# Reading a batch's edge scores out of an interleaved tile: a four-layer graph network on one Trainium2 core

## The chip, the cores and the metric

The kernel runs on one core of one Trainium2 chip (trn2). The metric is device microseconds of one execution, the median of three. The program is one launch; its input is in DRAM and so is its output.

## The reference, cut to what matters

Four graph layers run one after the other on `x`, which is 16 batches of 1024 nodes with 256 features, float32. All four use one 1024 by 1024 matrix `adj` that is mostly zeros (a random pattern, made symmetric, with the diagonal).

```
# layer 0
pre_u = h @ W1[:d];  pre_v = h @ W1[d:]
hidden = relu(pre_u[:, :, None, :] + pre_v[:, None, :, :] + b1)
S   = sigmoid(hidden @ W2 + b2)                      # (16, 1024, 1024): one score per batch and edge
a_t = einsum('buv,bud->bvd', S * A_a, h)             # the scored sums
m_t = einsum('uv,bud->bvd', A_m, h) * h
z   = beta1*h + beta2*(a_t @ Wa + ba) + beta3*(m_t @ Wm + bm)
# layer 1
z   = z + relu((A @ z) @ W.T + b)
# layers 2 and 3
feats = z @ W1.T;  f1 = feats @ W2 + b2
coefs = softmax(leaky_relu(f1[:, :, None] + f1[:, None, :]) + adj)
z   = coefs @ feats + bias2 + z
```

The change is in the line of `a_t`, the scored sums. `S * A_a` is zero where `adj` is zero, so the kernel works the scores out for the edges alone.

## The kernel before, in words

The 16 batches are worked in four groups of `GB` = 4. All matrices are cut into tiles of `P` = 128 nodes, so there are `NT` = 8 tiles of nodes.

A first stage finds for every node u the places and weights of its edges (up to 32) and makes, for the four batches of a group side by side, the two halves of the hidden layer, `u_d` and `v_d`, and `hw_d`, which is `h @ Wa`. If every node has few enough edges, the arm that starts at line 688 runs; the other arm (`arm.Else`) is a fallback that works on all pairs and isn't taken here.

The order of the work in that arm is written out by hand. Two streams are issued together by Python generators:

- The **side stream** (`score_steps`) makes the scores. One step gathers, for 128 nodes and one edge slot, the row of `v_d` of the neighbour (POOL, line 708), adds the row of u and multiplies (DVE, lines 825 and 827), sums over the features by four ACT activations (line 831), and at the end of a tile takes the sigmoid and multiplies by the edge's weight. Then the scores are scattered (POOL, line 713) into `dense`, a DRAM array of one row for each pair (u, v). **A row holds the four scores of the group's four batches, next to each other: 4 floats, 16 bytes.** There are two such arrays, for alternate groups.
- The **main stream** is the rest. For each group it is `with_edges` (the scored sums, and the only user of `dense`), and then `group_layers` (layers 1 to 3 of that group). `group_layers` of one group runs while the scores of the next one are made. Before the first group, the main stream does what needs no scores (`score_free`). After the last group's `with_edges` come `far_ahead` and `pair_layers`.

How far the side stream goes for each microsecond of the main stream is a constant of the place (`PACE`). `paced(ins, back)` makes an instruction wait for the matmul that was issued `back` products ago, so that no engine runs ahead of the plan. `product` is the helper through which nearly all matmuls go, at line 131, so that they all have this line in the profile.

**The scored sums, `with_edges`.** The output has the features on the partitions: for each batch i and half eh of the features, `acc[i][eh]` is a PSUM bank with 256 columns (`QN`), one for each node v of a block. There are four blocks of columns for each group, and for each block eight tiles `ut` of source nodes. One round of the inner loop takes one tile:

1. `load_gd` (line 907, issued by SP) brings the scores of 128 nodes u and 256 nodes v from `dense` into `gd`, a tile of 128 x 256 x 4 floats, in which the four batches are interleaved as in DRAM. The load is paced 24 products back, three rounds, and waits for the scatters of its group. The pool `gd` has four buffers.
2. ACT copies `gd` into `gc`, 128 x 4 x 256, in which each batch's 256 scores lie next to each other (line 1129). It reads every fourth float. It is paced 16 products back, two rounds. The pool `gc` has two buffers.
3. Eight products follow: for each of four batches and two halves, the stationary operand is a 128 x 128 piece of `hw[i]` and the moving operand is the 256 columns `gc[:, i, :]`. The profile shows two MATMUL and two LDWEIGHTS instructions for each product.

After eight rounds DVE adds the eight banks onto `z` (line 1152). Also issued in these rounds: loads of `z` and, in the first group, loads of the transposed `adj` and its exponential on ACT (line 1118). The first four `gd` tiles of a group are loaded ahead, while the layers of the group before it still run (`soon`).

In all there are 4 groups x 4 blocks x 8 tiles = 128 rounds, so 128 copies and 1024 products.

After the last `with_edges`, `by_lists` takes four tiles of the pool `gd` for another use (`msg`).

Of the kernel before, what the change touches and what calls it, by code (L numbers as in the profile page):

```python
# [11 lines left out]
F32 = mybir.dt.float32  # L12
I32 = mybir.dt.int32
U32 = mybir.dt.uint32
AF = mybir.ActivationFunctionType
ALU = mybir.AluOpType
AX = mybir.AxisListType
P = 128

GB = 4  # L20
# [23 lines left out]
def after(tc, ins, others, kind, why):  # L44
    dep = mybir.DependencyInfo(kind, mybir.DependencyReason.DATA)
    for o in others:
        tc.add_manual_dep(ins.ins, o.ins.name, dep, reason=why)
# [23 lines left out]
def gnn_stack_kernel(  # L71
# [27 lines left out]
    nc = tc.nc  # L99
# [6 lines left out]
    QN = HN // 2  # L106
# [6 lines left out]
    def bank():  # L113
        return psum[-1].tile([P, HN], F32, tag="bank", name="bank")

    def psum_pool(stack, name, bufs):
        psum.append(stack.enter_context(tc.tile_pool(name=name, bufs=bufs, space=bass.MemoryType.PSUM)))
        return psum[-1]
# [4 lines left out]
    def paced(ins, back=6):  # L123


        if recent:
            after(tc, ins, [recent[max(0, len(recent) - back)]], mybir.DependencyClass.Sync, "keeps pace")
        return ins

    def product(*args, **kw):  # L130
        recent.append(nc.tensor.matmul(*args, **kw))  # L131
        del recent[:-BACK]
        return recent[-1]
# [554 lines left out]
    with tc.If(listed > 0) as arm:  # L688
        with ExitStack() as stack:
# [8 lines left out]
            wide_z = stack.enter_context(tc.tile_pool(name="wide_z", bufs=4, reuse_waits="tile"))  # L698
            wide_t = stack.enter_context(tc.tile_pool(name="wide_t", bufs=5, reuse_waits="tile"))
            psum_pool(stack, "banks", 8)  # L700
            gd_pool = stack.enter_context(tc.tile_pool(name="gd", bufs=4, reuse_waits="tile"))
            gc_pool = stack.enter_context(tc.tile_pool(name="gc", bufs=2, reuse_waits="tile"))
            put = [Scatters(tc, f"scores {g}") for g in range(NGR)]
            finished = []
            TW = NT * (D + 1)
# [198 lines left out]
            def load_gd(g, v, ut, **pace):  # L904
                view = dense[g % BUFS][:DUMP].rearrange("(t p v) b -> t p v b", p=P, v=N)
                gd = gd_pool.tile([P, QN, GB], F32, tag="gd", name="gd")
                ins = nc.sync.dma_start(gd, view[ut][:, v * QN : (v + 1) * QN, :])
                put[g].before(paced(ins, **pace))
                return gd
# [207 lines left out]
            def exponential(jt):  # L1117
                paced(nc.scalar.activation(ea[:, jt, :], ea[:, jt, :], AF.Exp), 16)

            def with_edges(g, hw, z):  # L1120

                doing[0] = "edges"
                for v in range(N // QN):
                    cols = slice(v * QN, (v + 1) * QN)
                    acc = [[bank() for _ in range(DH)] for _ in range(GB)]
                    for ut in range(NT):
                        gd = first_gd.pop(0) if first_gd else load_gd(g, v, ut, back=BACK)
                        gc = gc_pool.tile([P, GB, QN], F32, tag="gc", name="gc")
                        paced(nc.scalar.activation(gc, gd.rearrange("p n i -> p i n"), AF.Copy), 16)  # L1129
                        for i in range(GB):  # L1130
                            for eh in range(DH):
                                product(
                                    acc[i][eh][:, :QN], hw[i][:, ut, eh * P : (eh + 1) * P], gc[:, i, :],
                                    start=ut == 0, stop=ut == NT - 1,
                                )
                        if z_loads and ut % 2 == 0:
                            load, i = z_loads.pop(0)
                            paced(load(i), 12)
                        if (to_load or to_exp) and ut % 2 and v:
                            if v > 1 and to_exp:  # L1140
                                exponential(to_exp.pop(0))
                            if to_load:
                                jt = to_load.pop(0)
                                paced(nc.sync.dma_start(ea[:, jt, :], adjT_d[jt]), 16)
                                to_exp.append(jt)
                        yield 3.4 if g or v else 1
                    if v == N // QN - 1:
                        while to_exp:
                            exponential(to_exp.pop(0))
                    for i in range(GB):  # L1150
                        for eh in range(DH):
                            nc.vector.scalar_tensor_tensor(
                                z[i][:, eh, cols], acc[i][eh][:, :QN], zbias[:, eh : eh + 1], z[i][:, eh, cols],
                                ALU.add, ALU.add,
                            )
# [264 lines left out]
            for g in range(NGR):  # L1420
                hw, z = loaded.pop(0)
                while g not in finished:
                    next(side.steps)
                side.along(with_edges(g, hw, z))
                if g < NGR - 1:
                    side.along(group_layers(g, z))
                else:
                    for _ in far_ahead(z[2:], pair_layers(g * GB, z[:2], layer_one(z[:2]))):
                        pass
                    for _ in pair_layers(g * GB + 2, z[2:], from_lists(z[2:], msg)):  # L1430
                        pass
# [131 lines left out]
```

## Time and profile before

| | |
|---|---|
| median of three runs | 3129.5 us (3126.07 to 3133.56) |
| the profiled execution, its own time | 3142.89 us |
| its span, first to last instruction | 3141.2 us |
| mean granted TensorE clock over the span | 0.995 |
| DVE busy | 2356.0 us, 75% |
| ACT busy | 1943.6 us, 62% |
| POOL busy | 1875.3 us, 60% |
| moved by DMA | 699.96 MB, 223 GB/s in the mean |

PE is TensorE's matmul, PEld its weight load, which overlaps it, and DVE, ACT, POOL and SP are the vector, scalar, GpSimd and sync engines. A row of the profile names the line, the engine, the operation, the tile written and the tiles read, the shapes, the number of instructions, then the busy time in us, the mean ns of one, the idle time of its engine just before them, and what ended that idle time. A busy share is an average over stages with different limits, so a change in one stage is read from that stage's own stretch of time.

The main stream passes through these stretches in the profiled execution: the first stage and `score_free` until 948 us; the scored sums of the four groups at 948.0 to 1069.1, 1501.7 to 1623.0, 2057.0 to 2182.8 and 2615.7 to 2726.2 us; `group_layers` in the three gaps between them, 432.6, 434.0 and 432.9 us long; and the end from 2726.2 to 3141.2 us.

### The profile page before, as it was taken

How to read it: one execution, taken by the hardware profiler on the slowest of the kernel's cores; microseconds unless marked ns; L12 is line 12 of the kernel's file. 1: busy time of each engine (PE TensorE's matmuls, PEld its weight loads, DVE VectorE, ACT ScalarE, POOL GpSimd, SP SyncE). 2: the span in 40 equal slices, each digit the busy share in tenths (PEclk: the TensorE clock that was granted, in tenths of full speed). 3: DMA queues.
4: the chain of work that ended last, by engine and by line, in shares of the span. 5: the costliest groups of instructions: out<-in, count | busy, mean ns of one | idle time of the engine just before them, and what ended most of it. 6: DMA issues, size and time to landing. Idle time of an engine off the chain costs nothing. (4 is left out here: it accounts for less than half of the span.)

```text
span 3141.2 us, 39031 instructions
## 1 busy us (share of the span) xinstructions
PE 3082.3 (98%) x11954; PEld 2182.9 (69%) x11954; DVE 2356.0 (75%) x3191; ACT 1943.6 (62%) x6512; POOL 1875.3 (60%) x1483
## 2 busy tenths in 40 slices
PE   9999999999999999999999999999999999999999
PEld 5444545545547756888775688878558888858888
DVE  7887778678774678999677899967789982157844
ACT  3245555566667876777887677778667764414242
POOL 1156778677674577777566776756777770076600
PEclk9999999999999999999999999999999999999999
DMA  9988898888889776568877765887775565485500
GB/s 322 332 321 311 271 293 270 264 253 243 260 288 332 228 215 203 155 187 291 266 228 203 215 164 165 271 266 235 217 212 167 157 200 168 133 256 159 161 4 28
DMA packets 288420, 699.96 MB, mean 223 GB/s; under 512 B 46141, under 2 KB 141178, under 8 KB 281034
## 3 DMA queue, kind: packets, MB, share of 16 engines
q0 software_dynamic: 128224, 387.80, 42.2%
q1 hardware_dynamic: 132538, 258.46, 24.0%
q10 hardware_dynamic: 27440, 51.13, 4.3%
q8 instruction: 96, 1.57, 0.2%
q14 instruction: 122, 1.00, 0.1%
HBM read 565.83 MB, written 131.41 MB: 222 GB/s over the span
## 5 line engine op out<-in xcount | busy, mean ns | idle before, releaser
L831 ACT ACTIVATE z<-z 128x256 f32<-128x256 f32 x2432 | 979.1, 406 | 543.3 <-DVE z L827 453.1
L825 DVE TENSOR_TENSOR z<-z,u 128x1024 f32<-128x1024 f32 x608 | 738.8, 1220 | 384.3 <-PE bank L131 267.6
L131 PE MATMUL bank<-feats,m 128*128 128x257 f32 x4096 | 909.1, 380 | 1.7 <-ACT feats L1016 1.1
L708 POOL DMA_INDIRECT z<-v_d,slot_v x512 | 663.1, 1295 | 404.6 <-ACT z L831 225.7
L131 PEld LDWEIGHTS bank<-feats,m 128*128 128x128 f32 x4096 | 769.3, 190 | 112.4 <-ACT feats L1016 1.9
L713 POOL DMA_INDIRECT dense_d<-gt,slot_at x512 | 665.3, 1299 | 184.6 <-issue 137.4
L827 DVE SCALAR_TENSOR_TENSOR z<-z,w2r 128x1024 f32<-128x1024 f32 x608 | 737.9, 1220 | 9.0
L131 PE MATMUL bank<-gc,hw 128*128 128x256 f32 x2048 | 456.6, 385 | 22.6 <-ACT gc L1129 13.9
L831 ACT ACTIVATION_READ_ACCUMULATOR z<-z 128x1 f32 x2432 | 461.5, 190 | 0.0
L131 PEld LDWEIGHTS bank<-gc,hw 128*128 128x128 f32 x2048 | 389.9, 192 | 88.8 <-ACT gc L1129 22.4
L131 PE MATMUL bank<-adj_sb,h 128*128 128x512 f32 x1024 | 443.6, 593 | 6.5 <-issue 2.8
L1099 DVE SCALAR_TENSOR_TENSOR m<-rho,tau,adj_sb 128x512 f32<-128x512 f32 x512 | 376.5, 744 | 66.5 <-PE bank L131 62.0
L131 PE MATMUL bank<-adjT_in,y 128*128 128x512 f32 (+1 forms) x960 | 403.7, 581 | 6.2 <-issue 3.8
L131 PEld LDWEIGHTS bank<-adj_sb,h 128*128 128x128 f32 x1024 | 194.6, 190 | 247.5 <-issue 242.0
L131 PEld LDWEIGHTS bank<-adjT_in,y 128*128 128x128 f32 x960 | 182.0, 191 | 221.4 <-issue 207.4
L131 PE MATMUL bank<-w,hT 128*128 128x512 f32 (+1 forms) x1024 | 334.8, 487 | 0.0
L1129 ACT ACTIVATE gc<-gd 128x1024 f32<-128x1024 f32 x128 | 264.9, 2071 | 101.0 <-PE bank L131 68.5
L131 PEld LDWEIGHTS bank<-w,hT 128*128 128x128 f32 x1024 | 194.8, 191 | 141.3 <-issue 122.5
L131 PE MATMUL bank<-g_wT,z 128*128 128x257 f32 x1024 | 231.1, 380 | 1.2 <-ACT st L1325 1.1
L131 PEld LDWEIGHTS bank<-g_wT,z 128*128 128x128 f32 x1024 | 192.0, 190 | 32.5 <-issue 3.3
L708 POOL DMA_INDIRECT z<-v_d,x_node x96 | 122.4, 1275 | 129.5 <-ACT z L831 99.5
L713 POOL DMA_INDIRECT dense_d<-gt,x_at x96 | 125.7, 1309 | 29.3 <-issue 27.4
(169 smaller groups left out, 2319.1 us busy)
## 6 DMA issues: line engine op xcount, KB each, us to landing
gd<-dense_d SPq DMA_DIRECT2D x128, 512.0 KB
dense_d<-zero ACTq DMA_DIRECT2D x64, 512.0 KB
adjT_in<-adjT_d SPq DMA_DIRECT2D x112, 256.0 KB
h<-in_x_dram SPq DMA_DIRECT2D x19, 1024.0 KB
u_d<-st SPq DMA_DIRECT2D x64, 256.0 KB
v_d<-st SPq DMA_DIRECT2D x64, 256.0 KB
hw_d<-st SPq DMA_DIRECT2D x64, 256.0 KB
u<-u_d POOLq DMA_DIRECT2D x32, 512.0 KB
```

Source lines behind the costliest of these rows:

```text
L131: recent.append(nc.tensor.matmul(*args, **kw))
L708: return nc.gpsimd.indirect_dma_start(out=dst, out_offset=None, in_=src[:], in_offset=bass.IndirectOffsetOnAxis(ap=at, axis=0), **how,)
L713: return nc.gpsimd.indirect_dma_start(out=dst[:], out_offset=bass.IndirectOffsetOnAxis(ap=at, axis=0), in_=src, in_offset=None,)
L825: paced(nc.vector.tensor_tensor(z, z, u, ALU.add))
L827: nc.vector.scalar_tensor_tensor(zk, zk, 0.0, w2r[:, None, :].to_broadcast([P, GB, D]), ALU.max, ALU.mult)
L831: nc.scalar.activation(zk[:, c, :], zk[:, c, :], AF.Copy, accum_out=s[:, k, c : c + 1])
L1099: nc.vector.scalar_tensor_tensor(m, r[:, cols], ta[:, kt : kt + 1], ea[:, kt, cols], ALU.max, ALU.mult)
L1129: paced(nc.scalar.activation(gc, gd.rearrange("p n i -> p i n"), AF.Copy), 16)
```

## The change

The copy into `gc` is taken out, with its pool. The products read batch i's scores straight from `gd`: the moving operand is `gd[:, :, i]`, 256 floats of which each lies 16 bytes after the one before it. The pool `gd` gets two more buffers, six in place of four.

```diff
-            gd_pool = stack.enter_context(tc.tile_pool(name="gd", bufs=4, reuse_waits="tile"))
-            gc_pool = stack.enter_context(tc.tile_pool(name="gc", bufs=2, reuse_waits="tile"))
+            gd_pool = stack.enter_context(tc.tile_pool(name="gd", bufs=6, reuse_waits="tile"))
...
                         gd = first_gd.pop(0) if first_gd else load_gd(g, v, ut, back=BACK)
-                        gc = gc_pool.tile([P, GB, QN], F32, tag="gc", name="gc")
-                        paced(nc.scalar.activation(gc, gd.rearrange("p n i -> p i n"), AF.Copy), 16)
                         for i in range(GB):
                             for eh in range(DH):
                                 product(
-                                    acc[i][eh][:, :QN], hw[i][:, ut, eh * P : (eh + 1) * P], gc[:, i, :],
+                                    acc[i][eh][:, :QN], hw[i][:, ut, eh * P : (eh + 1) * P], gd[:, :, i],
                                     start=ut == 0, stop=ut == NT - 1,
                                 )
```

The instructions of PE, DVE, POOL and SP stay the same in number and order. On ACT, the 128 copies are gone and everything else keeps its order. A tile of `gd` and one of `gc` have the same size (4 KB on each partition), so the six buffers take the room of the four and two.

## The prediction

> **What bounds the kernel now.** I read the page's busy times first, then its chain of waits, then the groups of instructions, then the stretches of the scored sums one by one, and last the time line of PE in the one group where nothing else runs.
>
> ```profile
> span 3141.2 us, 39031 instructions
> PE 3082.3 (98%) x11954; PEld 2182.9 (69%) x11954; DVE 2356.0 (75%) x3191; ACT 1943.6 (62%) x6512; POOL 1875.3 (60%) x1483
> ...
> DVE 0%; issue 0%
> ...
> L131 PE MATMUL bank<-gc,hw 128*128 128x256 f32 x2048 | 456.6, 385 | 22.6 <-ACT gc L1129 13.9
> L131 PEld LDWEIGHTS bank<-gc,hw 128*128 128x128 f32 x2048 | 389.9, 192 | 88.8 <-ACT gc L1129 22.4
> ...
> L1129 ACT ACTIVATE gc<-gd 128x1024 f32<-128x1024 f32 x128 | 264.9, 2071 | 101.0 <-PE bank L131 68.5
> ```
>
> PE is busy 98% of the span, so what doesn't shorten or lengthen PE's stream changes little. The chain that ended last holds only the last output piece and says nothing about this stage. The products of the scored sums keep PE busy for 456.6 us; PE is idle 22.6 us ahead of them, 13.9 of it for the copy. The copy costs ACT 264.9 us, but ACT is idle 38% of the span.
>
> ```profile
> 948.00:1069.10 121.10, 113.33 (x513) 96.09 (x512) 63.32 (x78) 103.28 (x208) 50.60 (x44) 1.00 0.89 306
> 1501.70:1623.00 121.30, 114.70 (x515) 97.83 (x514) 75.14 (x95) 105.95 (x246) 66.71 (x58) 0.97 0.81 259
> 2057.00:2182.80 125.80, 117.52 (x514) 99.04 (x513) 77.99 (x92) 104.93 (x243) 75.09 (x62) 0.96 0.81 257
> 2615.70:2726.20 110.50, 110.50 (x515) 97.27 (x514) 14.72 (x36) 62.01 (x31) 0.52 (x1) 1.00 0.48 150
> ```
>
> These are the four stretches (length, busy us of PE, PEld, DVE, ACT, POOL, then granted clock, DMA share, GB/s). Together they last 121.1 + 121.3 + 125.8 + 110.5 = 478.7 us. In the fourth, with no score work beside it, PE never stops:
>
> ```profile
> 2615.68 110.67 PE L131 MATMUL bank<-gc,hw 128*128 128x256 f32 x512
> 2726.19 13.98 PE L131 MATMUL bank<-l1wT,z 128*128 128x256 f32 x64
> ```
>
> The next group of matmuls starts 110.5 us after the first of 512, so one instruction takes 110.5 / 512 = 215.8 ns of PE's stream (the 385 ns of the row are of overlapping instructions), 0.843 ns a column. 2048 of them need 442.0 us without a wait; the stage lasts 478.7, so 36.7 us are waits and a lower clock. That is all that taking out the copy can win. Weight loads of 192 ns fit under 215.8 and are no bound.
>
> **The change part by part.**
>
> *Removed: 128 copies.* ACT loses 128 x 2.071 = 264.9 us that nothing waits for except PE's 13.9 us (and ACT's own successors, the score sums of line 831, which are paced by PE). I credit the 13.9 us and the slower clock and small gaps after such stops, 36.7 - 22.6 = 14.1 us, of which I leave about 3 us to the stops that remain. What remains of the idle time is 22.6 - 13.9 = 8.7 us, put down to issue and DVE: PE's two longest are 5.75 us at 1515.7, where the copy itself waited 4.6 us for a remote event (a score tile that landed late, as I read it), and 2.48 us at 2061.9 for an output piece. So 9 + 3 = 12 us of waits stay, and the gain is 36.7 - 12 = 24.7 us, between 0 and 36.7.
>
> *Added waits.* The products now wait for the load of `gd` where the copy did (17.3 us, 12 times, most of it not passed on to PE). The tile is needed one copy later, about 2.1 us, and the pacing of the load, three rounds or 3 x 16 x 0.2158 = 10.4 us ahead, is unchanged. Behind a PE that waits stand DVE's additions (line 1152) and the paced score work, none of it nearer to the end than PE. On SP the loads of `z`, `adj_sb` and `adjT_in` queue behind `gd`; these loads wait on PE already and keep their order. The buffer of `gd` is now let go by the round's last product, not by the copy; with six buffers that is the round six before, older than the pacing. I cost all this at nothing: the cover is those three rounds. If it went, the price is the landings that ACT saw late, 17.3 + 4.6 = 21.9 us, with 12 us of it already in the sum.
>
> *Changed: where the moving operand lies.* 2048 matmuls read 256 floats that lie 16 bytes apart. No matmul of the trace has such an operand, so the price must be bounded. The nearest row is the copy itself: ACT reading the same tile in the same pattern, against ACT reading 128x1024 floats in a row.
>
> ```profile
> L1129 ACT ACTIVATE gc<-gd 128x1024 f32<-128x1024 f32 x128 | 264.9, 2071 | 101.0 <-PE bank L131 68.5 <-DMA gd<-dense_d 17.3 <-issue 10.2
> L870 ACT ACTIVATE u<-b1r 128x1024 f32<-128x1024 f32 x56 | 58.8, 1050 | 31.5 <-DMA adjT_d<-stage 26.2 <-PE bank L131 4.0 <-DVE z L825 0.8
> L1078 ACT ACTIVATE rho<-rho 128x1024 f32<-128x1024 f32 x32 | 33.4, 1044 | 0.0
> ```
>
> The copy takes 2071 ns, 1.98 times the 1044 of line 1078; line 870 also runs through four rows of 256 and takes 1050, so it isn't the shape. It isn't contention either: in the fourth group, with the other engines nearly silent, the copy's mean is 2063. Between 256 and 1024 packed floats ACT's time grows from 406 to 1044 ns (lines 831 and 1078), 0.831 ns a float: the rate at which PE takes columns, 0.843. ACT wants a float at the same pace as PE and gets it at about half that pace when each is 16 bytes further on. Three values for PE:
> - nothing: 215.8 ns an instruction, 2048 x 0.2158 = 442 us;
> - ACT's ratio: 215.8 x 1.98 = 427.3 ns, 875 us;
> - ACT's extra time per float, (2071 - 1044) / 1024 = 1.003 ns, on 256 columns: 215.8 + 256.8 = 472.6 ns, 968 us.
>
> I take the ratio: the row is the same tile, the same step and the same pace. A price below nothing is excluded, since no other row of 256 columns is faster than this one.
>
> [...]
>
> **The sum.** 875 + 12 = 887 us in place of 478.7: 408 us more. The profiled execution's own 3142.9 us (1.7 more than its span) becomes 3551. The median of the runs stands at 3129.5 / 3142.89 = 0.9957 of it, so 3536 us. With the extra time per float: 968 + 12 - 478.7 = +501, 3644, and 3629 as a median. Outside the stage nothing pays it back: in the three stretches between, PE is busy 431.7 of 432.6, 432.1 of 434.0 and 432.1 of 432.9 us. The score work is issued at fixed places between the matmuls and waits longer with PE, so what is late next is nothing but PE.
>
> **The rivals.**
>
> 1. *PE reads scattered floats at no cost* (faster). [...] Against: ACT, at the same pace, loses half. Time: 442 + 12 - 478.7 = -24.7, that is 3118 and 3105 as a median; with all waits gone -36.7, 3093. It decides as long as an instruction stays below (478.7 - 12) / 2048 = 227.9 ns, 12 ns over today: 5.6% is all that PE's reads may lose.
> 2. *PE loses part*, because fetching the next float overlaps taking the last one better than in ACT. At half of the loss: (215.8 + 427.3) / 2 = 321.5 ns, 658 + 12 - 478.7 = +192, 3335 and 3320 as a median. Nothing in the profile speaks for a certain share; a sixth of the loss, about 252 ns, would give 3180.
> 3. *PE loses more than ACT*, if each of the two MATMUL instructions of a product fetched every float twice: above 3660. The packed row gives no sign of a second fetch.
>
> That the change doesn't do what it says I can exclude: the order of instructions shows ACT without its 128 copies and the same 2048 matmuls on `gd`.
>
> **How the numbers follow.** The forecast has 0.70, rival 1 0.18, rival 2 0.10 and rival 3 0.02. The predicted time is the forecast's 3536. Its own range is 3490 to 3660, from the ratio and the extra time per float, with 15 to 30 us for waits that go or come. The range shown reaches down through rival 2 to 3180 and leaves out rivals 1 and 3, 0.20 together. Measurement can tell 0.2%, 6 us, from no change: of rival 1, 0.17 is faster by more, 0.01 is not; the lowest 0.01 of rival 2 is the same too; the rest, 0.81, is slower.
>
> **What would show it.** The row of 2048 matmuls from `gd`, the four stretches, and above all the fourth group, which has no waits: 512 x 0.4273 = 219 us if the ratio holds, 242 with the extra time per float, 165 for half, 110.5 for nothing. The gaps between the groups should keep 432 to 434 us, ACT's busy time should fall by 265 us, and PE's wait for the copy be gone. A fourth group of 110 us would make the prediction wrong at its main step; gaps that shrink by more than some us would make the step "nothing pays it back" wrong.

## The result, and the profile after

The changed kernel takes 3590.9 us in the median of four runs (3587.9 to 3600.1), against 3127.8 us for the kernel before (four runs, 3124.5 to 3133.6): a ratio of 1.149, 95% interval 1.147 to 1.151. The time forecast was 3536 us. Here and below a ratio is the record's estimate from the single runs and need not equal the quotient of the two medians.

The page of the changed kernel: span, busy times, the chain, and two groups of instructions.

```profile
span 3586.1 us, 38830 instructions
PE 3553.3 (99%) x11954; PEld 2219.4 (62%) x11954; DVE 2364.0 (66%) x3191; ACT 1692.9 (47%) x6384; POOL 1854.9 (52%) x1483
...
DVE 0%; issue 0%
...
L131 PE MATMUL bank<-gd,hw 128*128 128x256 f32 x2048 | 928.5, 632 | 0.0
...
L131 PEld LDWEIGHTS bank<-gd,hw 128*128 128x128 f32 x2048 | 426.7, 209 | 499.4 <-issue 495.9
```

The same 2048 matmuls keep PE busy for 928.5 us in place of 456.6. PE waits for nothing ahead of them any more (0.0 in place of 22.6). ACT has 1692.9 us in place of 1943.6: the copies are gone. That is 250.7 us less, not the 265 that the prediction asks for. The prediction took the copies' own row, 264.9 us; but 13 us of that lies, in the records before, over other ACT instructions, which are still there. It doesn't help, since PE, the engine that bounds the kernel, is busy 99% of a longer span.

The four scored sums of the changed kernel, in the columns of the prediction's second fence (length, busy us of PE, PEld, DVE, ACT, POOL, clock, DMA share, GB/s), with one stretch of `group_layers` between the first two:

```profile
946.30:1178.20 231.90, 231.90 (x514) 106.81 (x513) 65.99 (x79) 46.73 (x180) 49.21 (x49) 1.00 0.51 164
1178.20:1610.80 432.60, 431.64 (x1810) 329.53 (x1809) 396.43 (x540) 312.75 (x1192) 317.75 (x232) 1.00 0.68 207
1610.80:1842.70 231.90, 231.90 (x515) 106.99 (x514) 76.96 (x95) 47.70 (x212) 62.70 (x61) 1.00 0.45 140
...
2275.30:2507.50 232.20, 232.20 (x514) 106.75 (x513) 81.71 (x96) 48.58 (x220) 65.91 (x63) 1.00 0.46 143
...
2940.60:3172.50 231.90, 231.90 (x514) 106.61 (x513) 16.44 (x36) 0.19 (x1) 0.52 (x1) 1.00 0.23 72
```

All four take 232 us, whether score work runs beside them (the first three) or not (the fourth). That alone says that no other engine and no transfer sets the time here. Together they last 927.9 us, 449.2 more than the 478.7 before. The span grew by 444.9, so nothing of it is paid back elsewhere beyond 4.3 us; the stretch between the first two groups is 432.6 us long, as before. One instruction takes 231.87 / 512 = 452.9 ns of PE's stream (first to first of the next group, as the prediction counted), 1.769 ns a column against 0.843.

### The profile page after: what moved, and what is told of

Same layout as the page of the kernel before. It is cut to its first block, busy times and chain, and to the rows that moved or that the text cites. A ratio compares the mean times of both kernels' runs of the same rounds, so it can differ in the third digit from the quotient of the medians.

```text
span 3586.1 us, 38830 instructions
## 1 busy us (share of the span) xinstructions
PE 3553.3 (99%) x11954; PEld 2219.4 (62%) x11954; DVE 2364.0 (66%) x3191; ACT 1692.9 (47%) x6384; POOL 1854.9 (52%) x1483
## 5 line engine op out<-in xcount | busy, mean ns | idle before, releaser
L707 POOL DMA_INDIRECT z<-v_d,slot_v x512 | 654.4, 1278 | 652.4 <-ACT z L830 515.7
L131 PE MATMUL bank<-gd,hw 128*128 128x256 f32 x2048 | 928.5, 632 | 0.0
L131 PEld LDWEIGHTS bank<-gd,hw 128*128 128x128 f32 x2048 | 426.7, 209 | 499.4 <-issue 495.9
L1149 DVE SCALAR_TENSOR_TENSOR z<-bank,zbias,z 128x256 f32<-128x256 f32 x128 | 60.5, 482 | 308.1 <-PE bank L131 307.6
L1167 ACT ACTIVATE y<-bank 128x512 f32<-128x512 f32 x64 | 37.8, 590 | 285.6 <-PE bank L131 285.4
```

Of the source, the lines that this page charges most:

```text
L707: return nc.gpsimd.indirect_dma_start(out=dst, out_offset=None, in_=src[:], in_offset=bass.IndirectOffsetOnAxis(ap=at, axis=0), **how,)
L1149: nc.vector.scalar_tensor_tensor(z[i][:, eh, cols], acc[i][eh][:, :QN], zbias[:, eh : eh + 1], z[i][:, eh, cols], ALU.add, ALU.add,)
L1167: nc.scalar.activation(y[i][:, jt : jt + 2, :], ps.rearrange("p (t d) -> p t d", t=2), AF.Copy)
```

## The experiments

The kernels that differ only in what the matmuls read were run once each, apart from the packed one. For all of them the time per instruction is read from the fourth scored sum, where PE never stops: the time from the first of its 512 matmuls to the first of the next group, over 512. "Beside it" means runs of the kernel before made together with the experiment; their median lies between 3139.5 and 3148.9 us, above the 3127.8 of the result, so an experiment is compared with those.

**Is it the step, or the tile that is read?** ACT still copies, but leaves the batches interleaved, with the buffers of before.

```diff
-                        gc = gc_pool.tile([P, GB, QN], F32, tag="gc", name="gc")
-                        paced(nc.scalar.activation(gc, gd.rearrange("p n i -> p i n"), AF.Copy), 16)
+                        gc = gc_pool.tile([P, QN, GB], F32, tag="gc", name="gc")
+                        paced(nc.scalar.activation(gc, gd, AF.Copy), 16)
...
-                                    acc[i][eh][:, :QN], hw[i][:, ut, eh * P : (eh + 1) * P], gc[:, i, :],
+                                    acc[i][eh][:, :QN], hw[i][:, ut, eh * P : (eh + 1) * P], gc[:, :, i],
```

> ACT still copies each loaded tile into gc, but without turning it, so that the products read every fourth float of a tile that ACT wrote, with the buffers of before. If the price lies in the 16-byte step of the moving operand: 2048 matmuls at about 453 ns, 928 us busy, as in the changed kernel, and 3560 to 3600 us in all; the copy itself falls from 2071 to about 1050 ns. If it lies in reading the tile that the DMA has filled, in the six buffers or in the missing copy: 216 ns an instruction, 442 to 457 us busy, about 3130 us.

Measured: 3593.2 us. Two groups of its profile:

```profile
L131 PE MATMUL bank<-gc,hw 128*128 128x256 f32 x2048 | 928.6, 632 | 0.1
...
L1129 ACT ACTIVATE gc<-gd 128x1024 f32<-128x1024 f32 x128 | 135.3, 1057 | 628.9 <-PE bank L131 397.7 <-issue 231.1
```

With copy and buffers back, the matmuls take the same 928.6 us. Neither the direct read of a loaded tile, nor the six buffers, nor the missing copy has a part in it. And the copy halves, from 2071 to 1057 ns, as soon as it reads in a row: the price has moved from ACT to PE.

**What is taking out the copy worth, without the step?** From the changed kernel, the products read packed floats.

```diff
+                        row = gd.rearrange("p n i -> p (n i)")
...
-                                    acc[i][eh][:, :QN], hw[i][:, ut, eh * P : (eh + 1) * P], gd[:, :, i],
+                                    acc[i][eh][:, :QN], hw[i][:, ut, eh * P : (eh + 1) * P], row[:, i * QN : (i + 1) * QN],
```

> No copy, six buffers as in the changed kernel, but the products read 256 floats in a row of the loaded tile (the scores of the wrong pairs: the values of the scored sums are not the reference's). If the step alone is the price: 216 ns an instruction, 442 us, and what the copy's absence is worth shows by itself: 3093 to 3117 us, forecast 3105. If reading the loaded tile directly is the price: 453 ns and about 3590 us. If the loads become the bound: waits of PE for gd of 15 us or more and 3125 us or above.

Measured: 3119.6 us against 3139.5 for the kernel before beside it, ratio 0.9940 (0.9925 to 0.9954). The row of its matmuls:

```profile
L131 PE MATMUL bank<-gd,hw 128*128 128x256 f32 x2048 | 446.1, 380 | 4.8 <-DVE st L1326 2.4 <-DMA gd<-dense_d 2.0 <-issue 0.2
```

The matmuls are busy 446.1 us, PE is idle 4.8 us ahead of them, 2.0 of that for loads of `gd`. So the gain of removing the copy is real, 14 to 24 us, a little less than the 24.7 us credited; and it is about the most that a way of feeding packed scores can win here, with only 4.8 us of idle time left.

**What does the price go by?** Four kernels change only which 256 floats are read (the values of the scored sums are then not the reference's). What the expectations call a line is 16 bytes on a partition, counted from the start of the tile; the text below calls it a piece. That the price would go by pieces of this size was the author's supposition, which these runs test. The diffs show the new text of the changed places; `...` stands for what is left out. The first two:

```diff
+                        row = gd.rearrange("p n i -> p (n i)")
+                        row = row.rearrange("p (n s) -> p n s", s=2)
...
+                                    ... row[:, i // 2 * QN : (i // 2 + 1) * QN, i % 2],
```

> As the changed kernel, but the products read every second float (8 bytes apart; the scores of the wrong pairs). If what costs is each new 16-byte line, 1.77 ns by the changed kernel, and two floats on a line share it: 0.885 ns a column, about 227 ns an instruction, 464 us, 3125 us in all. If the price grows evenly with the step (0.843 ns at one float, 1.771 at four): 1.152 ns, 295 ns, 604 us, 3265 us. If any step above one float is read at half speed: 453 ns, 928 us, 3590 us.

```diff
+                        row = gd.rearrange("p n i -> p (n i)")
+                        row = row[:, : 3 * QN].rearrange("p (n s) -> p n s", s=3)
...
+                                    ... row[:, :, i % 3],
```

> As the changed kernel, but the products read every third float (12 bytes apart; the scores of the wrong pairs). Four such floats lie on three 16-byte lines. If each new line costs 1.77 ns: 1.33 ns a column, 340 ns an instruction, 696 us, 3355 us in all. If the price grows evenly with the step: 1.46 ns, 374 ns, 766 us, 3425 us. If the step is free below 16 bytes: 216 ns, 442 us, 3105 us.

Then a step of 32 bytes, and pairs of neighbours whose beginnings lie 32 bytes apart:

```diff
+                                    ... hw[i].rearrange("p t d -> p (t d)").rearrange("p (n s) -> p n s", s=8)[:, :, ut],
```

> As the changed kernel, but the moving operand is every eighth float (32 bytes apart) of the tile hw, in place of the scores. If each new 16-byte line costs 1.77 ns and how far the lines lie apart doesn't matter: 453 ns an instruction as at 16 bytes, 928 us, about 3590 us in all. If the price goes on growing with the step: 1.239 ns more than a packed float for four more floats of step, 3.0 ns a column, 770 ns an instruction, some 1577 us, 4230 us. The loads of gd stay, but nothing reads them.

```diff
+                        row = gd.rearrange("p n i -> p (n i)")
+                        row = row.rearrange("p (n s) -> p n s", s=8)
...
+                                    acc[i][eh][:, :QN].rearrange("p (n s) -> p n s", s=2), ... row[:, :, 2 * i : 2 * i + 2],
```

> As the changed kernel, but the products read pairs: two floats in a row, then a gap of six, so that pairs begin 32 bytes apart and each line that is touched is hit twice (the scores of the wrong pairs). If only hits for each line count: 227 ns an instruction, 465 us, 3125 to 3145 us in all, as with every second float. If each jump in the pattern costs what a jump of 16 bytes costs: (0.843 + 1.77) / 2 = 1.31 ns a column, 335 ns, 685 us, 3345 us.

The fourth scored sum on PE's time line (start, length, instructions), of every second float, of every third, of the pairs, and of every eighth:

```profile
2609.66 115.79 PE L131 MATMUL bank<-gd,hw 128*128 128x256 f32 x512
2725.30 13.97 PE L131 MATMUL bank<-l1wT,z 128*128 128x256 f32 x64
```

```profile
2770.01 174.03 PE L131 MATMUL bank<-gd,hw 128*128 128x256 f32 x512
2943.87 13.98 PE L131 MATMUL bank<-l1wT,z 128*128 128x256 f32 x64
```

```profile
2617.66 117.82 PE L131 MATMUL bank<-gd,hw 128*128 128x256 f32 x512
2735.32 9.87 PE L131 MATMUL bank<-l1wT,z 128*128 128x256 f32 x45
```

```profile
2962.53 236.11 PE L131 MATMUL bank<-hw 128*128 128x256 f32 x512
3198.46 11.84 PE L131 MATMUL bank<-l1wT,z 128*128 128x256 f32 x54
```

The difference of the two starts over 512, beside the number of 16-byte pieces that 256 such floats touch:

| moving operand | pieces of 16 bytes | ns an instruction | ns a piece | time, us |
|---|---|---|---|---|
| packed | 64 | 215.8 | (3.37) | 3119.6 |
| every second float | 128 | 225.9 | 1.765 | 3141.3 |
| pairs, 32 bytes apart | 128 | 229.8 | 1.795 | 3151.0 |
| every third float | 192 | 339.6 | 1.769 | 3359.3 |
| every fourth (the change) | 256 | 452.9 | 1.769 | 3590.9 |
| every eighth | 256 | 460.8 | 1.800 | 3616.1 |

The last column compares only roughly: the kernel before took 3139.5 us beside the packed, second and third floats, 3148.9 beside the pairs and the eighth floats, and 3127.8 beside the change. Every second float came 16 us above the total expected and the pairs 6 us above the top of theirs, though their instructions took the 227 ns expected within 3 ns; the totals were reckoned from 3105 us for packed operands, which took 3119.6.

One number describes the table within 2%: an instruction takes 215.8 ns or 1.77 ns for each piece that it touches, whichever is longer. Every third float was the sharpest test, since the three readings were 70 us and more apart: 340 ns was expected by pieces, 374 by an even rise with the step, 216 if only a step of 16 bytes counted; 339.6 came out. Why a piece costs PE this much isn't shown by these runs. What falls: that any step halves the speed (every second float), that the price goes on rising with the step beyond 16 bytes (every eighth), that each jump costs (the pairs). Pieces that begin 32 bytes apart cost 1.7% more than pieces 16 bytes apart (460.8 against 452.9 ns). Every eighth float is also read from another tile, `hw`; but the pairs, read from `gd`, show the same 1.7% over every second float (229.8 against 225.9 ns), which points to the distance and not to the tile.

The size of 16 bytes is borne out too. With pieces of 8 bytes every second float would touch 256 of them, as many as every fourth, but the two took 225.9 and 452.9 ns. With pieces of 32 bytes every fourth would touch 128 and every eighth 256, but they took 452.9 and 460.8 ns.

**Does a weight load pay as well?** The operands are exchanged; the sums come out with nodes on the partitions.

```diff
-                                    acc[i][eh][:, :QN], hw[i][:, ut, eh * P : (eh + 1) * P], gd[:, :, i],
+                                    acc[i][eh][:, :QN], gd[:, eh * P : (eh + 1) * P, i], hw[i][:, ut, :],
```

> As the changed kernel, but with the operands exchanged: the weight load takes 128 of the scores, every fourth float of gd, and the moving operand is 256 packed floats of hw, so that the sums come out with the nodes on the partitions; they are added to z as if they had not been turned, so the values are not the reference's. If a weight load also pays 1.77 ns for each line: 128 x 1.77 = 227 ns in place of 190, hidden or nearly hidden beside 216 ns of matmul, 442 to 480 us, 3105 to 3145 us in all. If a weight load at this step takes twice its time: 380 ns, no longer hidden, 778 us, about 3440 us.

Measured: 3157.0 us, with 3148.9 for the kernel before beside it. Its two groups, and the fourth scored sum on PE's time line:

```profile
L131 PE MATMUL bank<-hw,gd 128*128 128x256 f32 x2048 | 484.4, 399 | 3.7 <-DVE st L1325 1.4 <-DMA gd<-dense_d 1.4 <-DVE z L1149 0.7
L131 PEld LDWEIGHTS bank<-hw,gd 128*128 128x128 f32 x2048 | 481.2, 330 | 6.7 <-DMA gd<-dense_d 2.0 <-issue 1.9 <-DVE z L1149 1.3
```

```profile
2620.91 120.16 PE L131 MATMUL bank<-hw,gd 128*128 128x256 f32 x512
2740.91 13.98 PE L131 MATMUL bank<-l1wT,z 128*128 128x256 f32 x64
```

The weight loads now fill the stage, 481.2 us or 235 ns each, 1.84 ns a float; packed ones took 190. One weight load with its matmul takes 120.0 us / 512 = 234.4 ns in the fourth sum, so the weight load sets the pace in place of the 215.8 ns of the matmul. The total is 12 us above the range of the first reading and the stage 4 us above it; the second reading, 380 ns, is far off. That a weight load pays by the piece, like the moving operand, fits (1.84 against 1.77 ns) but rests on this one step. There are only 128 floats in a load, and 216 ns of matmul hide nearly all of it. Against the 446.1 us of packed operands, the same scores cost 38 us as the stationary operand and 482 (928.5) as the moving one. It is no finished kernel, since the sums would have to be turned back.

**Can the 0.6% be had with packed operands?** Five versions of the kernel before, which all keep a turned copy. First, a third buffer for the copies (the smaller changes that this brings, three tiles loaded ahead and the four tiles of `msg`, are left out of the diff):

```diff
-            gd_pool = stack.enter_context(tc.tile_pool(name="gd", bufs=4, reuse_waits="tile"))
-            gc_pool = stack.enter_context(tc.tile_pool(name="gc", bufs=2, reuse_waits="tile"))
+            gd_pool = stack.enter_context(tc.tile_pool(name="gd", bufs=3, reuse_waits="tile"))
+            gc_pool = stack.enter_context(tc.tile_pool(name="gc", bufs=3, reuse_waits="tile"))
```

> The kernel before with three buffers for the turned copy gc and three for gd (three tiles of a group loaded ahead, not four; the four tiles that are used again at the end come two from each pool). If PE's waits for the copy come from its having only two buffers, so that a copy can't start before the products of two rounds ago are done: PE's 13.9 us of waits for the copy fall under 4 us and the time by 8 to 18 us, to 3112 to 3122 us against 3130. If they come from ACT's other work ahead of the copy, or if the lost fourth load hurts: 3125 us or above, with waits for loads of gd in their place.

Measured: 3141.7 against 3148.9 us, ratio 0.9987 (0.9970 to 1.0003).

```profile
L131 PE MATMUL bank<-gc,hw 128*128 128x256 f32 x2048 | 452.3, 382 | 22.6 <-ACT gc L1129 15.6 <-DVE st L1331 4.2 <-issue 2.3
L1129 ACT ACTIVATE gc<-gd 128x1024 f32<-128x1024 f32 x128 | 263.3, 2068 | 87.6 <-PE bank L131 52.8 <-DMA gd<-dense_d 34.7
```

PE waits 15.6 us for copies, not under 4, so a third buffer alone doesn't help. This doesn't yet clear the two buffers: the copies now wait 34.7 us for loads of `gd`, 17.3 before, since a buffer was taken from there, and the pace still holds each copy back until a product of two rounds ago. The last two versions below keep two buffers and lose most of the waits, which does clear them. Next, every second copy on DVE:

```diff
-                        paced(nc.scalar.activation(gc, gd.rearrange("p n i -> p i n"), AF.Copy), 16)
+                        turning = gd.rearrange("p n i -> p i n")
+                        if ut % 2:
+                            paced(nc.vector.tensor_copy(gc, turning), 16)
+                        else:
+                            paced(nc.scalar.activation(gc, turning, AF.Copy), 16)
```

> The kernel before with every second copy made by DVE in place of ACT (64 copies each). If PE's waits for the copy come from how much ACT has to do in the scored sums (it is busy without a gap at 1040 to 1060 us of the kernel before): these waits fall from 13.9 to under 6 us and the time by 6 to 15 us, 0.2 to 0.5%. If they come from where the copy stands in the queue, behind score work that waits itself: DVE's queue has the same waits, PE waits as long as before, and the time stays within 5 us. DVE's own copy at this step has no row yet: 1.77 ns a float would make it 1.8 to 2.0 us.

Measured: 3136.3 against 3141.8 us, ratio 0.9970 (0.9950 to 0.9989). The matmuls, and the two engines' copies of such tiles, in one profile:

```profile
L131 PE MATMUL bank<-gc,hw 128*128 128x256 f32 x2048 | 452.4, 383 | 22.9 <-ACT gc L1133 9.3 <-DVE gc L1131 5.0 <-issue 4.7
L1133 ACT ACTIVATE gc<-gd 128x1024 f32<-128x1024 f32 x64 | 132.8, 2075 | 171.2 <-PE bank L131 126.3 <-DMA gd<-dense_d 26.2 <-issue 17.1
L1131 DVE COPY gc<-gd 128x1024 f32<-128x1024 f32 x64 | 71.4, 1116 | 105.6 <-PE bank L131 84.4 <-DMA gd<-dense_d 18.8 <-issue 2.2
```

DVE needs 1116 ns where ACT needs 2075, against 1.8 to 2.0 us expected. The time fell, by the ratio as the first reading says, but PE still waits 9.3 + 5.0 = 14.3 us for copies, as the second says, so neither reading is borne out whole. Then the place in the queue: the copy of the next round is issued ahead of this round's products and of the score work that follows them.

```diff
+                rounds = [(v, ut) for v in range(N // QN) for ut in range(NT)]
+                copies = []
+                def turn():
+                    w, t = rounds.pop(0)
+                    gd = first_gd.pop(0) if first_gd else load_gd(g, w, t, back=BACK)
+                    gc = gc_pool.tile([P, GB, QN], F32, tag="gc", name="gc")
+                    paced(nc.scalar.activation(gc, gd.rearrange("p n i -> p i n"), AF.Copy), 16)
+                    copies.append(gc)
+                turn()
...
-                        gd = first_gd.pop(0) if first_gd else load_gd(g, v, ut, back=BACK)
-                        gc = gc_pool.tile([P, GB, QN], F32, tag="gc", name="gc")
-                        paced(nc.scalar.activation(gc, gd.rearrange("p n i -> p i n"), AF.Copy), 16)
+                        if rounds:
+                            turn()
+                        gc = copies.pop(0)
```

> The kernel before with each copy, and the load ahead of it, issued one round earlier, ahead of the products and the score work of the round before. If the copy's place in ACT's queue makes PE wait: the 13.9 us fall under 4 us, and the time comes near the 19 us that the packed operands without a copy gained, 3 of them kept back: a ratio of 0.994 to 0.997. If ACT's amount of work is the limit: half of that or less, 0.997 to 1.000.

Measured: 3137.8 against 3141.8 us, ratio 0.9988 (0.9974 to 1.0002), which falls in the second reading's range.

```profile
L131 PE MATMUL bank<-gc,hw 128*128 128x256 f32 x2048 | 454.6, 384 | 18.8 <-ACT gc L1130 8.9 <-issue 7.4 <-DVE st L1339 1.9
```

The waits for copies fell from 13.9 to 8.9 us, by about a third, not under 4. Alone it is inconclusive. Both together (the diff is against the version just shown):

```diff
-                    paced(nc.scalar.activation(gc, gd.rearrange("p n i -> p i n"), AF.Copy), 16)
+                    turning = gd.rearrange("p n i -> p i n")
+                    if t % 2:
+                        paced(nc.vector.tensor_copy(gc, turning), 16)
+                    else:
+                        paced(nc.scalar.activation(gc, turning, AF.Copy), 16)
```

> Both: copies a round earlier and every second one on DVE. If both the amount and the place in the queue count: a ratio of 0.993 to 0.996, as good as no copy at all. If one of them is all there is: the same as the better of the two alone, within 0.1%.

Measured: 3123.6 us against 3141.8, ratio 0.9941 (0.9919 to 0.9963). That is in the first reading's range. Its interval overlaps that of the alternate copies alone (0.9950 to 0.9989), so that both count is likely rather than shown. And with `turn` making all copies on DVE (the diff again against the copies a round early):

```diff
-                    paced(nc.scalar.activation(gc, gd.rearrange("p n i -> p i n"), AF.Copy), 16)
+                    paced(nc.vector.tensor_copy(gc, gd.rearrange("p n i -> p i n")), 16)
```

> All 128 copies on DVE, a round early. The alternate copies have shown that DVE takes 1.06 to 1.12 us for one, half of ACT's 2.07. If the copies' total time is what matters: 128 x 1.1 = 141 us in place of 265, PE's waits for copies under 5 us and a ratio of 0.993 to 0.996, as with copies shared between both. If DVE, which has 63 to 78 us of work in each of the first three scored sums already, becomes what ACT was (35 us more in each, and its additions onto z wait for PE): waits for the copies of 6 us or more, and 0.997 to 1.000.

Measured: 3128.8 against 3144.7 us, ratio 0.9942 (0.9919 to 0.9965). The matmuls and the copies of these two versions, copies shared and copies on DVE alone:

```profile
L131 PE MATMUL bank<-gc,hw 128*128 128x256 f32 x2048 | 447.9, 381 | 9.1 <-ACT gc L1134 3.8 <-DVE st L1343 3.2 <-issue 1.3
L1134 ACT ACTIVATE gc<-gd 128x1024 f32<-128x1024 f32 x64 | 133.0, 2078 | 152.3 <-PE bank L131 88.4 <-issue 45.2 <-DMA gd<-dense_d 13.5
L1132 DVE COPY gc<-gd 128x1024 f32<-128x1024 f32 x64 | 71.6, 1119 | 91.3 <-PE bank L131 76.5 <-DMA gd<-dense_d 9.3 <-issue 5.6
```

```profile
L131 PE MATMUL bank<-gc,hw 128*128 128x256 f32 x2048 | 447.9, 381 | 7.9 <-issue 4.1 <-DVE gc L1130 2.3 <-DVE z L1163 0.6
L1130 DVE COPY gc<-gd 128x1024 f32<-128x1024 f32 x128 | 142.7, 1116 | 89.0 <-PE bank L131 78.3 <-DMA gd<-dense_d 8.6 <-issue 2.0
```

The waits for copies are down to 3.8 and 2.3 us, and both versions are as fast as having no copy at all (0.9940). They beat the kernel before by 0.6% and the changed one by about 13%. The intervals of the two overlap almost wholly, so which one is better stays open; DVE alone needs less work, 142.7 us of copies in place of 133.0 + 71.6. All copies on DVE without the earlier place weren't run, so whether the place is needed there isn't known.

## Why the prediction was right

**Moving operand** (the step that decides): right in kind, mis-sized as a term. "ACT's ratio: 215.8 x 1.98 = 427.3 ns, 875 us" was taken, 452.9 ns and 927.9 us came, between it and the other bound, "472.6 ns, 968 us". This term was 52 us short (2048 x 25.6 ns). Two errors in it partly cancelled, so its nearness is in part luck. First, the ratio also scales ACT's fixed part, the 193 ns that an instruction takes whatever its length (an estimate, 1044 - 1024 x 0.831, from lines of two different operations). Taken as a time per piece, the copy with 1024 pieces gives (2071 - 193) / 1024 = 1.83 ns, or 469 ns for 256 pieces, 42 more than the ratio. Second, PE's own price is 1.77 ns a piece, which takes 17 ns off again. The bound should have been read as an interval between pieces that replaces the column's 0.843 ns; at a step of four the sum gives nearly the same (472.6 ns), but every second float, where nearly nothing is added (225.9 against 215.8 ns), shows that it is an interval.

That ACT's row could stand for PE at all was also luck as far as the record goes: the prediction gave no reason but the same tile, step and pace, and DVE, on the same tiles at the same step, takes 1116 ns and not 2071. The trace of the kernel before, which has no matmul with such an operand, left this open, and rival 1 with its 0.18 covered it.

**Waits that stay**, 12 us: none stayed. With PE at 452.9 ns an instruction in place of 215.8 the loads and the other engines' work are always there in time (idle 0.0 us), so 12 us of the 52 came back: 887 us were forecast for the stage, 927.9 measured, 41 us more. The gain of 24.7 us for the copy was near: 14 to 24 us with packed operands, where 4.8 us of waits stay.

**Added waits at nothing**: right within 2 us. With packed operands read straight from `gd`, where they would show, PE waits 2.0 us for loads.

**Nothing pays it back**: right; 449.2 us in the stage are 444.9 us in the span, and the three gaps are 432.6, 432.6 and 433.1 us long.

**The scale to the median**: the profiled execution was forecast at 3551 us and took 3587.9. Going from 3551 to 3536 took off 15 us for a profiled execution of before that was slower than its median; that of the changed kernel is 3 us faster than its median. Mis-sized stage and scale together are the 55 us between 3536 and 3590.9.

**Rivals.** That PE reads scattered floats at no cost is refuted by the change itself and by the interleaved copy, which keeps a copy and the buffers of before: 928.6 us. The break-even of 227.9 ns is nearly reached: every second float, at 225.9 ns, stays just under it, and its time of 3141.3 us is about that of the kernel before beside it (3139.5). That PE loses only part of what ACT loses is refuted at step four; at step three the time does lie in between, but by the number of pieces (192 of them, 339.6 ns) and not by an overlap. That PE loses more through a second fetch is refuted by the time, 3590.9 and not above 3660 us; the two MATMUL instructions of a product also cost the same, 453.4 and 452.4 ns in the mean over the fourth sum.

## What to carry to other kernels

Ask of every operand of a matmul how many 16-byte pieces of SBUF it touches on a partition: as the moving operand of this kernel each cost 1.77 to 1.80 ns where it gave one or two floats, so 256 float32 columns on 256 such pieces took 2.1 times their packed time (452.9 against 215.8 ns), and two floats on a piece were nearly free (225.9 ns, 5% more). The copy that packs the operand was worth keeping here, where each score is streamed four times (two halves, two MATMUL instructions each) and the copying engine has time that PE, the bounding engine, hasn't (ACT 62% busy, PE 98%); with fewer reads it wasn't tried. Look first for the engine that copies it cheapest, and try the copy ahead of work that waits (here that helped together with DVE; alone it was inconclusive). A row of another engine on the same tile with the same step is a candidate for a price that the trace doesn't hold, not a bound: with its fixed part taken off, ACT's came within 4% of PE's (1.83 against 1.77 ns a float), but DVE's, 1.04 to 1.09 with the fixed part in it, is far from both. Measuring the price itself, as the runs above do, is surer.

## What the runs showed of the hardware that was not expected

DVE reads such a tile faster than PE or ACT: 1.06 us at best and 1.12 in the mean for 1024 floats 16 bytes apart, 1.04 to 1.09 ns a float, less than the 1.77 of PE and the 1.83 of ACT. So 1.77 ns a piece doesn't hold for every reader. That DVE pays nothing for the step isn't shown: no run has its packed copy of such a tile. A row of the kernel before with one packed input, though of another operation, speaks for some price:

```profile
L164 DVE TENSOR_SCALAR w<-w,beta 128x512 f32<-128x512 f32 x2 | 1.0, 483 | 9.6 <-DMA w<-in_L_gnn_Wa_dram 9.6
```

It takes 483 ns for 512 floats, 0.94 ns a float with its fixed part in it.

The fourth scored sums agree with the 1.77 ns within 0.3% at steps of two, three and four, without any fixed part for an instruction; the weight load, at 1.84 ns a float, is close to the 1.83 of ACT.
